# The order of VectorE's work within one step of an interleaved 30-pass FFN

## The chip, the cores and the metric

The kernel runs on one core of a Trainium2 chip. The core has a matrix engine (TensorE, PE in the profile, with PEld for its weight loads), VectorE (DVE), ScalarE (ACT), GpSimd (POOL) and SyncE (SP), each with its own instruction queue worked in order, and 16 DMA engines. The metric is the device time of one execution in microseconds (us), lower is better; the median of three runs of the kernel before is 4197.89 us (4197.65 to 4198.25).

## The reference

One layer of a graph network over 12500 nodes with 256 features in float32. A graph convolution and a linear attention are added to the input; then a feed-forward recurrence of 30 passes is applied to every node. Cut to what matters here:

```python
xn = _layernorm(x)
x = x + relu(segment_sum((xn @ weight)[src] * edge_weight, dst)) + linear_attention(xn)

def step(h, _):                       # 30 times
    h = h + 0.01 * jnp.tanh(h)
    h = h * jax.nn.sigmoid(h)         # silu
    h = _layernorm(h, ln_w, ln_b)
    h = jnp.einsum('bsc,dc->bsd', h, W) + b
    return (h, None)

x = x + scan(step, _layernorm(x), length=30)
```

The rows are independent in the 30 passes. Within a row each pass needs the one before it.

## The kernel before

The 12500 nodes lie in 98 tiles of 128 rows, and these in 25 groups of four tiles (the last group has two). The kernel first norms x, builds edge lists and the attention's sums; from about 0.42 ms on, one long loop mixes everything that is left: the attention's product (`mix`) and the convolution's product (`W`) of each group, the edge sums that feed it, and the 750 passes (25 groups by 30).

A planner, `plan()`, lists the steps of that loop in the program beforehand. Each step has at most one item: `mix`, `W` or a `pass` of one group. Up to five groups are in their passes at once (ABREAST), two passes of one group stand at least four steps apart (APART), and a step may also hold two quads of edge sums, some gathers, and the joining of a new group. The list has 803 steps: 750 passes, 25 `mix`, 23 `W` and 5 empty ones. The instructions are then written in the order of the loop, and that order is kept on each engine's queue (`manual_schedule`).

A pass is a software pipeline over steps. If the pass is the item of step k:

- before it, `normed` (L1017 on, its instruction at L1022) makes z, the normed activations, with four VectorE instructions, one a tile. It is written in the first step in which the group's statistics exist and its pass is one or two steps ahead.
- step k: `transposes` on TensorE (L1036, into `pt`), and `copies` on ScalarE (L1043, to `zT`).
- step k+1: `matrix`, 16 matmuls (L1049) into `po`, of which there are two buffers.
- step k+2: `act1`, a Tanh on ScalarE (L995); `act2`, on VectorE s = 0.01 * tanh + h (L1001) and on ScalarE the Silu (L1002); `stats`, two `bn_stats` on VectorE (L1008) and on GpSimd ve (L1012) and rs, a power (L1014).

After the 30th pass the result is added to the base rows instead (L1108) and sent out by SyncE's queue. `mix` and `W` items end two steps later with sums on VectorE (L1114, L1123, L1124).

At the top of a step VectorE gets the selection matrices of coming quads (`selections`, L210 to L223) and clears a slot of the edge sums (L276). ScalarE copies the quads' sums (L247) and the finished slot (L275) ahead of the Tanh. GpSimd's gathers (L184) are written after the matmuls, behind the rs of the step before and ahead of this step's ve.

A group joins over six steps, held in the list `fresh` by the step k3 of its start: statistics of its base rows (L1174, L1178, L1180) in k3 and k3+1, its first norm (L1146, L1153, L1157) and Tanh in k3+2 and k3+3, its `act2` in k3+4, its `stats` at the end of k3+5.

So VectorE's order in a step of before is: selections, clearing; s of the pass two steps back (or a sum into the base); a joining group's s; z of the passes due in the next two steps; a joining group's first norm; the `bn_stats` of the pass two steps back; a joining group's statistics.

Of the kernel before, what the change touches and what calls it, by code (L numbers as in the profile page):

```python
# [31 lines left out]
def gps_layer(  # L32
# [252 lines left out]
    class KeyValue:  # L285
# [19 lines left out]
        def normed(self):  # L305
            rs8 = kvw.tile([P, 2 * HEADS], F32, name="rs8")
            nc.vector.reciprocal(rs8, self.sd)
            nc.vector.tensor_tensor(
                kns[self.t % 3][:, :, :D], self.pkv, rs8[:, :, None].to_broadcast([P, 2 * HEADS, D]), ALU.mult
            )  # L310
# [315 lines left out]
    with tc.If(n_out > 0):  # L626
        with ExitStack() as pg_:
# [12 lines left out]
            for t in range(NE):  # L640
# [8 lines left out]
                d = gp.tile([P, 1], F32, name="d")  # L649
                nc.vector.tensor_copy(d[:rows], d_i[:rows])  # L650
                d = d[:rows]
# [333 lines left out]
    norm, zs, zTs, pos, xts, first_norm = {}, {}, {}, {}, {}, {}  # L985
# [3 lines left out]
    def flat(h, nt):  # L989
        return h[:, : nt // 2].rearrange("p q c j -> p (q c j)")  # L990
# [7 lines left out]
    def act2(gi, h, s):  # L998
        nt = groups[gi][1]
        sf = flat(s, nt)  # L1000
        nc.vector.scalar_tensor_tensor(sf, sf, 0.01, flat(h, nt), op0=ALU.mult, op1=ALU.add)  # L1001
        nc.scalar.activation(sf, sf, AF.Silu)  # L1002

    def stats(gi, s):
        t0, nt = groups[gi]
        st = hp.tile([P, G // 2, 6], F32, name="st")
        for q in range(nt // 2):
            nc.vector.bn_stats(st[:, q, :], s[:, q].rearrange("p c j -> p (c j)"))  # L1008

        sv = st.rearrange("p q (j f) -> p (q j) f", f=3)  # L1010
        ve = fp.tile([P, G], F32, name="ve")
        nc.gpsimd.tensor_scalar(ve[:, :nt], sv[:, :nt, 2], 1.0 / C, EPS, ALU.mult, ALU.add)  # L1012
        rs = hp.tile([P, G], F32, name="rs")
        nc.gpsimd.tensor_tensor(rs[:, :nt], ve[:, :nt], mhalf[:, :nt], ALU.pow)  # L1014
        norm[gi] = (s, sv, rs)
# [41 lines left out]
    item = lambda k: steps[k][0] if 0 <= k < K and steps[k][0] else (None, None)  # L1057
    quads_of = lambda k: steps[k][1] if k < K else 0
    fresh = []
    written = {}  # L1060
    selections(ed.summed + quads_of(0) - ed.selected)
    for k in range(K + 3):
        nq = quads_of(k)

        selections(ed.summed + nq + quads_of(k + 1) - ed.selected)
        copy_quads()
        free_nodes()
        kind, gi = item(k)[:2]
        if kind in ("mix", "W"):
            t0, nt = groups[gi]  # L1070
            xts[kind, gi] = fp.tile([P, G, C], F32, name="xt")
            if kind == "mix":
                load_rows(x, xts[kind, gi], t0, nt, nc.sync)
            else:
                rows = accw[bass.ds(n_out * ((G + t0) * P), nt * P), :]
                nc.sync.dma_start(out=xts[kind, gi][:, :nt, :], in_=rows.rearrange("(g p) c -> p g c", p=P))

        if kind == "pass":
            transposes(gi)
        kind1, g1 = item(k - 1)[:2]  # L1080

        if kind1 == "pass":
            zT, _ = zTs.pop(g1)
            pos[kind1, g1] = matrix(groups[g1][1], lambda j, k: zT[:, j, k, :], w2, True)
        elif kind1 == "mix":
            pos[kind1, g1] = matrix(groups[g1][1], lambda j, k: xnT[g1][:, j, k, :], mix)
        elif kind1 == "W":
            aT = ed.aT.pop(g1)
            pos[kind1, g1] = matrix(groups[g1][1], lambda j, k: aT[:, k, j * P : (j + 1) * P], wg)
        add_quads()  # L1090
        gathers(steps[k][3] if k < K else 0)
        for _ in range(nq):
            sum_quad()

        kind2, g2 = item(k - 2)[:2]
        last = kind2 == "pass" and item(k - 2)[2] == FFN_ITERS - 1
        if kind2 == "pass" and not last:
            s2 = act1(g2, pos[kind2, g2])
        if kind == "pass":
            copies(gi)  # L1100
        if kind2 == "pass" and not last:
            act2(g2, pos.pop((kind2, g2)), s2)
        elif last:
            t0, nt = groups[g2]
            for q in range(nt // 2):
                h = pos[kind2, g2][:, q].rearrange("p c j -> p j c")
                r = slice(2 * q, 2 * q + 2)
                nc.vector.tensor_tensor(base[g2][:, r, :], h, base[g2][:, r, :], ALU.add)  # L1108
            pos.pop((kind2, g2))
            rows_io(out, base[g2], t0, nt, False, nc.sync)  # L1110
            written[g2] = k
        elif kind2 == "mix":
            nt = groups[g2][1]
            nc.vector.tensor_tensor(base[g2], pos.pop((kind2, g2))[:, :nt, :], xts.pop((kind2, g2))[:, :nt, :], ALU.add)  # L1114
            if g2 < ed.weighted:
                aT = ed.aT.pop(g2).rearrange("p k (g n) -> p k g n", n=P)
                for i in range(KC):
                    bk = base[g2][:, :, i * P : (i + 1) * P]
                    nc.vector.scalar_tensor_tensor(bk, aT[:, i], 0.0, bk, op0=ALU.max, op1=ALU.add)
        elif kind2 == "W":  # L1120
            nt = groups[g2][1]
            ac = xts.pop((kind2, g2))[:, :nt, :]
            nc.vector.tensor_tensor(ac, pos.pop((kind2, g2))[:, :nt, :], ac, ALU.add)  # L1123
            nc.vector.scalar_tensor_tensor(base[g2], ac, 0.0, base[g2], op0=ALU.max, op1=ALU.add)  # L1124

        for g3, k3 in fresh:
            if k == k3 + 4:
                act2(g3, *first_norm[g3])  # L1130
        for d in (1, 2):
            kind3, g3 = item(k + d)[:2]
            if kind3 == "pass" and g3 in norm:
                normed(g3)
        for g3, k3 in fresh:
            nt = groups[g3][1]
            if k in (k3 + 2, k3 + 3):
                mv, rs = first_norm[g3, "stats"]
                if k == k3 + 2:

                    if 0 in written and written[0] + 2 <= k:
                        h = base[0].rearrange("p g c -> p (g c)").rearrange("p (q c j) -> p q c j", c=C, j=2)
                    else:
                        h = fp.tile([P, G // 2, C, 2], F32, name="z", bufs=3)
                    sh = fp.tile([P, G], F32, name="f_ve")
                    nc.vector.scalar_tensor_tensor(  # L1146
                        sh[:, :nt], mv[:, :nt, 0], -1.0, rs[:, :nt], op0=ALU.mult, op1=ALU.mult
                    )
                    first_norm[g3, "h"] = (h, sh)
                h, sh = first_norm[g3, "h"]  # L1150
                q = k - k3 - 2
                if 2 * q < nt:
                    nc.scalar.activation(  # L1153
                        h[:, q, :, 0], base[g3][:, 2 * q, :], AF.Identity, bias=sh[:, 2 * q : 2 * q + 1],
                        scale=rs[:, 2 * q : 2 * q + 1],
                    )
                    nc.vector.tensor_scalar(  # L1157
                        h[:, q, :, 1], base[g3][:, 2 * q + 1, :], mv[:, 2 * q + 1, 0:1], rs[:, 2 * q + 1 : 2 * q + 2],
                        ALU.subtract, ALU.mult,
                    )  # L1160
                if k == k3 + 3:
                    first_norm[g3] = (h, act1(g3, h))
        if kind2 == "pass" and not last:
            stats(g2, s2)
        start = steps[k][2] if k < K else None
        if start is not None:
            fresh.append((start, k))
        for g3, k3 in list(fresh):
            nt = groups[g3][1]
            if k == k3:  # L1170
                first_norm[g3, "st"] = fp.tile([P, G, 6], F32, name="f_st")
            for j in range(nt):
                if j // 2 == k - k3:
                    nc.vector.bn_stats(first_norm[g3, "st"][:, j, :], base[g3][:, j, :])  # L1174
            if k == k3 + 1:
                mv = fp.tile([P, G, 2], F32, name="f_mv")
                for j in range(nt):
                    nc.vector.bn_aggr(mv[:, j, :], first_norm[g3, "st"][:, j, :])  # L1178
                ve = fp.tile([P, G], F32, name="f_ve")
                nc.vector.tensor_scalar(ve[:, :nt], mv[:, :nt, 1], 1.0, EPS, ALU.mult, ALU.add)  # L1180
                rs = fp.tile([P, G], F32, name="f_rs")
                nc.gpsimd.tensor_tensor(rs[:, :nt], ve[:, :nt], mhalf[:, :nt], ALU.pow)
                first_norm[g3, "stats"] = (mv, rs)
            elif k == k3 + 5:
                stats(g3, first_norm[g3][1])
                fresh.remove((g3, k3))
# [31 lines left out]
```

## Time and profile before

| | |
|---|---|
| median of 3 runs | 4197.89 us |
| profiled execution, its time | 4203.52 us |
| its span | 4201.7 us |
| granted TensorE clock, mean | 0.99 |
| z (L1022), 2940 instructions | 1033.1 us busy |
| st (L1008), 1470 | 938.1 us busy |
| s (L1001) out of po, 725 | 863.8 us busy |
| Silu (L1002), 750 | 780.5 us busy |
| Tanh (L995) out of po, 725 | 729.7 us busy |
| rs (L1014), 750 | 763.7 us busy |
| gathers (L184), 1563 | 1596.3 us busy |

A line of the timeline gives the start, the length, engine, line, operation, the tile written and those read, the shapes and how many instructions are merged; in brackets the idle time before it and what ended it. A line of the waits gives who waited for whom, the total, how many times and the longest. A line of the windows gives the stretch, its length, the busy time of PE, PEld, DVE, ACT and POOL (with the number of instructions), the granted clock, the DMA share and GB/s.

### The profile page before, as it was taken

What the parts mean: (1) busy time and instruction counts of PE and PEld (TensorE: products, weight loads), DVE (VectorE), ACT (ScalarE), POOL (GpSimd) and SP (SyncE); (2) the same over time, 40 slices, a digit from 0 to 9 for tenths busy, and PEclk for the clock granted to TensorE, in tenths of its full rate; (3) what the DMA queues carried; (4) which work ended last, traced back from release to release, by engine and by line L of the source; (5) the groups of instructions that cost most, each with busy time, mean ns of one, the idle gap of its engine ahead of it and who ended that gap; (6) DMA issues with size and microseconds to landing.
All of it is one profiled execution on the core that took longest, in us unless ns stands there. A gap on an engine that the chain in (4) does not pass through costs nothing.

```text
span 4201.7 us, 68013 instructions
## 1 busy us (share of the span) xinstructions
PE 4074.6 (97%) x24201; PEld 3383.3 (81%) x24201; DVE 3400.9 (81%) x7393; ACT 2525.7 (60%) x3762; POOL 2575.3 (61%) x3186
## 2 busy tenths in 40 slices
PE   8797999999999999999999999999999999999999
PEld 4444778888888888888888888888888888888888
DVE  8454578888888888888888888888888888888887
ACT  7332246666666666666666666666666665667775
POOL 3464666777777777777777777777667652222222
PEclk9899999999999999999999999999999999999999
DMA  8322532222222222222222222222222210000000
GB/s 261 102 87 71 154 97 66 64 62 64 76 61 71 75 64 72 72 66 71 72 64 72 78 64 72 71 73 60 72 70 59 64 49 14 6 6 1 1 1 23
DMA packets 147687, 278.36 MB, mean 66 GB/s; under 512 B 28047, under 2 KB 97197, under 8 KB 147341
## 3 DMA queue, kind: packets, MB, share of 16 engines
q0 software_dynamic: 75024, 204.97, 16.8%
q1 hardware_dynamic: 72173, 68.42, 5.3%
q8 instruction: 197, 3.23, 0.3%
q14 instruction: 149, 1.22, 0.1%
q10 hardware_dynamic: 144, 0.52, 0.0%
HBM read 247.68 MB, written 26.12 MB: 65 GB/s over the span
## 4 chain that ended last, share of the span: by engine, by line
PE 77%; DVE 11%; ACT 3%; issue 3%; POOL 2%; another core or an unknown queue 1%; DMA 0%; POOLq 0%; ACTq 0%; DVEq 0%
PE po L1049 53%; PE pt L1036 13%; PE pq L236 4%; DVE z L1022 4%; PE pa L261 3%; PE pkv L290 3%; DVE st L1008 3%; DVE s L1001 2%; ACT s L995 1%; POOL rs L1014 1%; PE pacc L316 1%; ACT s L1002 1%; POOL xg L184 0%; DVE big L1108 0%
## 5 line engine op out<-in xcount | busy, mean ns | idle before, releaser
L1049 PE MATMUL po<-w,zT 128*128 128x256 f32 x11760 | 2670.7, 380 | 3.7 <-ACT zT L1043 1.8
L1049 PEld LDWEIGHTS po<-w,zT 128*128 128x128 f32 x11760 | 2179.6, 190 | 282.9 <-issue 7.8
L184 POOL DMA_INDIRECT xg<-xnd,src_i x1563 | 1596.3, 1021 | 529.8 <-issue 317.6
L1002 ACT ACTIVATE s<-s 128x1024 f32<-128x1024 f32 (+1 forms) x750 | 780.5, 1041 | 580.2 <-DVE s L1001 561.3
L1022 DVE TENSOR_SCALAR z<-s,st,rs 128x256 f32<-128x256 f32 x2940 | 1033.1, 417 | 94.5 <-POOL rs L1014 90.8
L1008 DVE BATCH_NORM_STATS2 st<-s 128x6 f32<-128x512 f32 x1470 | 938.1, 679 | 181.8 <-ACT s L1002 163.6
L1001 DVE SCALAR_TENSOR_TENSOR s<-s,po 128x1024 f32<-128x1024 f32 x725 | 863.8, 1192 | 269.1 <-ACT s L995 207.0
L995 ACT ACTIVATE s<-po 128x1024 f32<-128x1024 f32 x725 | 729.7, 1007 | 216.8 <-PE po L1049 205.6
L1043 ACT ACTIVATE zT<-pt 128x512 f32<-128x512 f32 x1470 | 801.8, 602 | 60.9 <-PE pt L1036 57.3
L1036 PE MATMUL pt<-ident,z 128*128 128x128 f32 x5880 | 793.9, 276 | 36.1 <-DVE z L1022 34.3
L1036 PEld LDWEIGHTS pt<-ident,z 128*128 128x128 f32 x5880 | 671.1, 142 | 174.7 <-issue 78.6
L1014 POOL TENSOR_TENSOR rs<-ve,mhalf 128x4 f32<-128x4 f32 (+1 forms) x750 | 763.7, 1018 | 62.5
L1012 POOL TENSOR_SCALAR ve<-st 128x4 f32<-128x4 f32 (+1 forms) x750 | 146.8, 196 | 946.5 <-DVE st L1008 899.3
L247 ACT COPY sq<-pq 128x256 f32<-128x256 f32 x196 | 72.4, 370 | 296.2 <-PE pq L236 196.1
L236 PE MATMUL pq<-xg,sel 128*32 128x256 f32 x3126 | 224.0, 386 | 9.1 <-issue 7.0
L290 PE MATMUL pkv<-wkv,big 128*128 128x512 f32 x392 | 199.3, 631 | 10.2 <-issue 5.4
L261 PE MATMUL pa<-selq,sq 128*128 128x192 f32 (+2 forms) x1168 | 182.7, 293 | 13.6 <-ACT sq L247 9.2
L261 PEld LDWEIGHTS pa<-selq,sq 128*128 128x128 f32 x1168 | 170.8, 192 | 25.0 <-ACT sq L247 10.0
L275 ACT COPY aT<-pa 128x128 f32<-128x128 f32 x196 | 51.5, 263 | 213.9 <-PE pa L261 147.3
L236 PEld LDWEIGHTS pq<-xg,sel 128*32 128x32 f32 x3126 | 84.9, 109 | 112.8 <-issue 71.9
L301 DVE TENSOR_REDUCE v<-sq 128x8 f32<-128x512 f32 x98 | 66.8, 682 | 95.1 <-ACT sq L297 77.8
L290 PEld LDWEIGHTS pkv<-wkv,big 128*128 128x128 f32 x392 | 70.3, 198 | 67.4 <-issue 57.6
(154 smaller groups left out, 1532.0 us busy)
## 6 DMA issues: line engine op xcount, KB each, us to landing
xg<-xnd,src_i POOLq DMA_INDIRECT x1563
xt<-in_x_dram SPq DMA_DIRECT2D x48, 512.0 KB
xnd<-xt SPq DMA_DIRECT2D x24, 512.0 KB
out_dram<-big SPq DMA_DIRECT2D x24, 512.0 KB
xt<-accw SPq DMA_DIRECT2D x22, 512.0 KB
ac<-accw SPq DMA_DIRECT2D x2, 512.0 KB
xg<-in_dst_dram SPq DMA_DIRECT2D x6, 128.0 KB
xg<-in_src_dram SPq DMA_DIRECT2D x6, 128.0 KB
```

The costliest lines, as they stand in the source:

```text
L184: nc.gpsimd.indirect_dma_start(out=ed.xg[t], out_offset=None, in_=xnd, in_offset=bass.IndirectOffsetOnAxis(ap=src_i[:, t : t + 1], axis=0),)
L236: nc.tensor.matmul(ed.pq[j * 2 * WIN : (j + 1) * 2 * WIN, :], lhsT=sel[:, j, :], rhs=ed.xg.pop(q * Q + j), start=(q % 2 == 0), stop=last, ...
L261: nc.tensor.matmul(pa[:, k, c : c + hi - lo], lhsT=sq[:rows, k * P : (k + 1) * P], rhs=selq[:rows, lo - n0 : hi - n0], start=False, stop=( ...
L995: nc.scalar.activation(flat(s, nt), flat(h, nt), AF.Tanh)
L1001: nc.vector.scalar_tensor_tensor(sf, sf, 0.01, flat(h, nt), op0=ALU.mult, op1=ALU.add)
L1002: nc.scalar.activation(sf, sf, AF.Silu)
L1008: nc.vector.bn_stats(st[:, q, :], s[:, q].rearrange("p c j -> p (c j)"))
L1014: nc.gpsimd.tensor_tensor(rs[:, :nt], ve[:, :nt], mhalf[:, :nt], ALU.pow)
L1022: nc.vector.tensor_scalar(z[:, j, :], s[:, j // 2, :, j % 2], sv[:, j, 1:2], rs[:, j : j + 1], ALU.subtract, ALU.mult)
L1036: nc.tensor.transpose(pt[:, i, k, :], z[:, 2 * q + i, k * P : (k + 1) * P], ident)
L1043: nc.scalar.activation(zT[:, 2 * q : 2 * q + 2], pt, AF.Copy, bias=1.0)
L1049: nc.tensor.matmul(po[:, j // 2, :, j % 2] if paired else po[:, j, :], lhsT=lhsT(j, k), rhs=rhs[:, k, :], start=(k == 0 and (j % 2 == 0 or ...
```

## The change

Two blocks of the loop are moved; no instruction is added or taken away. The block that norms the passes due in the next two steps goes from behind the activations' sums to ahead of them, directly after TensorE's work of the step is written. The sum of a joining group (with its Silu) goes from ahead of the norms to behind the statistics of the pass two steps back.

```diff
@@ -1092,6 +1092,11 @@
         for _ in range(nq):
             sum_quad()
 
+        for d in (1, 2):
+            kind3, g3 = item(k + d)[:2]
+            if kind3 == "pass" and g3 in norm:
+                normed(g3)
+
         kind2, g2 = item(k - 2)[:2]
         last = kind2 == "pass" and item(k - 2)[2] == FFN_ITERS - 1
         if kind2 == "pass" and not last:
@@ -1126,13 +1131,6 @@
 
 
         for g3, k3 in fresh:
-            if k == k3 + 4:
-                act2(g3, *first_norm[g3])
-        for d in (1, 2):
-            kind3, g3 = item(k + d)[:2]
-            if kind3 == "pass" and g3 in norm:
-                normed(g3)
-        for g3, k3 in fresh:
             nt = groups[g3][1]
             if k in (k3 + 2, k3 + 3):
                 mv, rs = first_norm[g3, "stats"]
@@ -1162,6 +1160,9 @@
                     first_norm[g3] = (h, act1(g3, h))
         if kind2 == "pass" and not last:
             stats(g2, s2)
+        for g3, k3 in fresh:
+            if k == k3 + 4:
+                act2(g3, *first_norm[g3])
         start = steps[k][2] if k < K else None
         if start is not None:
             fresh.append((start, k))
```

VectorE's order in a step becomes: selections, clearing; z of the passes due in the next two steps; s of the pass two steps back (or a sum into the base); a joining group's first norm; the `bn_stats` of the pass two steps back; a joining group's s; a joining group's statistics.

## The prediction

> **What bounds the kernel now.** I read four views: the page (busy shares, chain), the windows over the long stage, the timeline, and the waits of VectorE and TensorE. First the page and the window from 640 to 4177 us.
>
> ```profile
> span 4201.7 us, 68013 instructions
> PE 4074.6 (97%) x24201; PEld 3383.3 (81%) x24201; DVE 3400.9 (81%) x7393; ACT 2525.7 (60%) x3762; POOL 2575.3 (61%) x3186
> PE 77%; DVE 11%; ACT 3%; issue 3%; POOL 2%; another core or an unknown queue 1%; DMA 0%; POOLq 0%; ACTq 0%; DVEq 0%
> 640.00:4177.00 3537.00, 3504.01 (x20999) 3007.25 (x20998) 3000.01 (x6298) 2269.57 (x3242) 2223.29 (x2754) 1.00 0.19 55
> ```
>
> The chain of work that ended last runs mainly on PE, and in the window PE is busy 3504 of 3537 us at clock 1.00, DVE 3000. So PE sets the pace and DVE has 537 us to spare. What matters is how those spare microseconds are arranged, and that is read in the timeline. Two stretches: a steady one with gathers, and a late one with gaps in it.
>
> ```profile
> 2009.54 1.27 DVE L1008 BATCH_NORM_STATS2 st<-s 128x6 f32<-128x512 f32 x2
> 2010.90 0.19 POOL L1012 TENSOR_SCALAR ve<-st 128x4 f32<-128x4 f32 x1
> 2011.18 1.04 POOL L1014 TENSOR_TENSOR rs<-ve,mhalf 128x4 f32<-128x4 f32 x1
> 2012.08 1.21 DVE L1001 SCALAR_TENSOR_TENSOR s<-s,po 128x1024 f32<-128x1024 f32 x1
> 2013.20 1.38 DVE L1022 TENSOR_SCALAR z<-s,st,rs 128x256 f32<-128x256 f32 x4
> 2014.48 1.28 DVE L1008 BATCH_NORM_STATS2 st<-s 128x6 f32<-128x512 f32 x2
> ```
> ```profile
> 3882.11 1.22 DVE L1001 SCALAR_TENSOR_TENSOR s<-s,po 128x1024 f32<-128x1024 f32 x1
> ...
> 3883.36 1.06 ACT L1002 ACTIVATE s<-s 128x1024 f32<-128x1024 f32 x1 [0.31 <-DVE s L1001]
> ...
> 3884.45 1.29 DVE L1008 BATCH_NORM_STATS2 st<-s 128x6 f32<-128x512 f32 x2 [1.12 <-ACT s L1002]
> ...
> 3885.83 0.20 POOL L1012 TENSOR_SCALAR ve<-st 128x4 f32<-128x4 f32 x1 [2.38 <-DVE st L1008]
> 3886.11 1.01 POOL L1014 TENSOR_TENSOR rs<-ve,mhalf 128x4 f32<-128x4 f32 x1
> ...
> 3887.15 1.39 DVE L1022 TENSOR_SCALAR z<-s,st,rs 128x256 f32<-128x256 f32 x4 [0.82 <-POOL rs L1014]
> ```
>
> A step's DVE work is a ring: s feeds the Silu on ACT, the Silu feeds the statistics st, st feeds ve and rs on POOL, rs feeds z. The first stretch shows the order of before hiding both hand-overs: while POOL makes rs (2010.90 to 2012.22) DVE works on selections and s; while ACT does the Silu, DVE does z, and st starts with no gap. The second stretch shows both hand-overs bare: no z is due behind s at 3882.11, so st idles 1.12 us for the Silu, and z at 3887.15 comes 1.41 us after st ended at 3885.74, although a half-size s lies between. The waits:
>
> ```profile
> DVE s L1001 <- ACT s L995: 207.0, 212, 5.2
> DVE st L1008 <- ACT s L1002: 163.6, 155, 1.9
> DVE z L1022 <- POOL rs L1014: 90.8, 214, 2.1
> PE pt L1036 <- DVE z L1022: 34.3, 39, 2.4
> ```
>
> Columns are total us, times, longest. DVE's largest wait is for the Tanh, that is for PE. PE waited for z only 34.3 us in all, so the most that earlier z's can give back is about that.
>
> **The change part by part.** It adds and removes no instruction, and what it moves issues no DMA and nothing on POOL or SP; a moved sum carries one Silu on ACT.
>
> (1) Norms to the front of the step. The z's now stand on DVE ahead of s, and behind the statistics of the step before. A pass at step k has its statistics at step k+2, and at step k+3 a z is due if the group's next pass is at k+4 or k+5. The planner keeps passes of a group at least 4 steps apart and has five groups abreast, so that is the usual case. I followed the planner's list through the loop: 803 steps, 750 passes (725 with s and st), 750 z's; 565 z's fall in the step right after their statistics, in 549 different steps. In each of those DVE now meets st, then z, with only selections between, and waits the whole 1.41 us for rs. And s no longer has a z behind it: each st waits the 1.12 us of the Silu, as at 3884.45. So both covers go at once, and DVE's ring closes once a step:
> z to s 1.30 (2013.20 to 2014.48 is 1.28, 3887.15 to the next DVE instruction 1.31) + s to st uncovered 2.34 (3882.11 to 3884.45) + st 1.28 + st's end to z 1.41 = 6.33 us, against 4.71 us that a step takes now (3554 us over the 754 steps number 40 to 793, whose ends follow).
>
> The sum from step 40 (its matmuls begin at 622.6) to step 793 (DVE's first last-pass sum of the tail, 4176.7); ranks in the plan counted, prices from the timeline rows:
> - s, Silu, st: 679 x (2.34 + 1.28) = 2458; the last group has half the tiles: 28 x (1.38 + 0.69) = 58, from its rows at 4188 to 4190 us (s, 1.38 later st of 0.69)
> - z: 700 x 1.30 = 910; half-size 28 x 0.65 = 18 (six z parts take 2.03, four 1.38)
> - waits for rs: 504 x 1.41 = 711; half-size 27 x 1.09 = 29 (st ends 4161.60, ve 4161.69, rs 4161.97 for 0.69)
> - sums into the base in steps that have no s: 6 x 1.13 + 21 x 2.38 + 20 x 1.20 = 81
> - selections of a pair of quads, 1.27 each: about 110 pairs fall in steps with an rs wait and lie inside its 1.41, so they cost nothing; the other 51 cost 65. If the cover were absent: 140 more.
> - 167 steps have no z; there s follows st so soon that the Tanh, queued on ACT behind the Silu and sometimes a copy, is late: about 20.
> Together 4350 (2516 + 928 + 740 + 81 + 65 + 20).
>
> (2) A joining group's sum (s and Silu) at the end of the step, 22 joinings in this stretch. Its DVE 1.13 lies in the rs wait of the next step in 21 cases, but its Silu (1.06) now stands on ACT ahead of the next Tanh (1.02) with st already done: from the end of st 1.25 + 1.06 + 1.05 = 3.4 until s may start, against 1.41 + 1.30 = 2.7. The bounds are 0 and 22 x 1.2; I take 26, the side of the rows. The joining group's own st at the end of the step costs 22 x 1.20 = 26, and its other statistics 10 that no rs wait covers. Together 62.
>
> (3) POOL. Behind rs it issues gathers, some 1.26 from one to the next (2008.56, 2009.82), mostly two or three a step. In a 6.33 us step three fit (3.8 us) before the next ve is due 4.9 us after rs. In a step without z (3.62 us) they do not, and rs comes late for the following z. The trace of before does not run at this pace; bounds 0 and one gather for each of some 120 such steps, 150 us; I take 40, since two gathers just fit with the small waits of (1).
>
> (4) PE. z earlier gives at most its 34.3 us, and that only if PE were still the bound. PE needs about 4.7 us a step, the ring 4452 / 754 = 5.9 on the mean, so PE idles some 1.2 us a step and the gain is nothing. PSUM: s and the base sums free the matmul's buffers later on DVE; two buffers give two rings, 11 us, for 3.6 us of matmuls and 1.05 of Tanh, so it costs nothing; without that cover up to the ring again.
>
> Sum: 622.6 + 4350 + 62 + 40 + 25 (4176.7 to 4201.7, the end, unchanged) = 5100 us of span, 898 above 4201.7. The profiled execution took 4203.5, 5.6 above the median of 4197.9; the same difference gives 4197.9 + 898, about **5095 us**, a factor 1.21.
>
> Two rules were weighed against this. In the page's first lines PE is the fullest engine, and DVE has a fifth of its time free. The Trainium skill (Perfetto Trace Analysis, Identifying the Most-Contended Engine) ranks engines by occupancy and would have PE optimised first, from which an order on DVE should be worth about nothing, and 4198 us would stay. The timeline's ring decides otherwise for me. The second is the clock. The granted clock in the rows:
>
> ```profile
> 340.00:360.00 20.00, 16.98 (x99) 9.47 (x100) 11.59 (x30) 6.33 (x16) 12.26 (x14) 1.00 0.29 85
> 400.00:420.00 20.00, 15.69 (x91) 12.68 (x92) 9.54 (x26) 0.64 (x2) 6.08 (x7) 0.78 0.23 61
> 420.00:440.00 20.00, 15.28 (x51) 7.68 (x50) 0.17 (x1) 0.90 (x4) 12.77 (x14) 0.65 0.42 128
> ```
>
> With short gaps and PE 85% busy the clock is 1.00; around and after a 12.8 us idle stretch (before 403.7) it is 0.78 and 0.65. The new PE gaps are short, under 2 us, so I take 1.00. The Trainium skill (TensorE: Matmul & The Clock Gate, HAM oscillation) puts the limit at idle gaps of about 3.4 us, and by that too nothing is added; at the half rate that it states for longer gaps PE would need 9.4 us a step and bind.
>
> **The rivals.**
> - POOL late everywhere (0.13): a gather, 1.26 us, stands before ve in the steps with an rs wait, as where st ended at 2004.45 and ve came at 2005.68. In half of them 549/2 x 1.26 = 345 more, 5440; in all 5790. Against it: the longer step has room.
> - Half the rs waits covered (0.10): if more than selections lay between st and z, 0.5 x 740 less, about 4725. For it: joinings and base sums; against it: they are counted, and are few.
> - The clock falls (0.03). PE would bind below 4.71 / 5.9 = 0.80 of full clock. At 0.65 it is 7.25 us a step, 754 x 1.35 = 1020 more, about 6110.
> - Not slower (0.03), the other side: rs is ready before z is reached. Then z's at the front cost nothing, PE's 34.3 us of waiting for z goes, and the time is 4164. My sum has 740 us of rs waits and 780 for Silu and Tanh, 2.0 us a step, and 3.9 for the rest of the ring; it decides where ring and PE are equal, at 0.8 us of waits a step. Against it: DVE already waits 90.8 us for rs in spite of an s in between.
>
> **How the numbers follow.** The forecast has 0.71; its own range is 4980 to 5230, from (2) and (3) at their bounds and the tanh waits of the steps without z at 0 to 0.5 us each. To leave out no more than 2 in 10 the range goes to 4900, part of the way to the covered case, and 5370, a POOL late in about two fifths of the steps. Within 0.2% (8 us, about what can be told from no change here) I give 0.01, faster 0.02, slower 0.97.
>
> **What would show it.** In the profile after: PE busy share near 80%; idle before z put down to rs of some 600 to 750 us; idle before st put down to the Silu of some 750 us; DVE's wait for the Tanh small; the chain mainly on DVE, ACT and POOL; a timeline of z, s, gap 1.1, st, gap 1.4. It is wrong if z's do not wait for rs, if the Silu is still covered, or if the clock column falls.

## The result, and the profile after

The changed kernel takes 5176.1 us (median of 4; 5170.85 to 5178.91), the kernel before 4198.1 beside it: a ratio of 1.2325, 95% interval 1.2311 to 1.2339, 978 us slower. The forecast was 5095, with a range of 4900 to 5370. The profiled execution took 5175.53 us, its span is 5173.7.

The page of the changed kernel, the lines that answer to those shown of before (span, busy times, and the chain by engine and by line):

```profile
span 5173.7 us, 67124 instructions
PE 4397.8 (85%) x24201; PEld 3496.6 (68%) x24201; DVE 3437.6 (66%) x7393; ACT 2471.5 (48%) x3762; POOL 2617.9 (51%) x3186
DVE 47%; POOL 16%; PE 15%; ACT 12%; issue 6%; another core or an unknown queue 0%; POOLq 0%; DMA 0%; DVEq 0%; ACTq 0%
DVE z L1022 17%; DVE st L1008 14%; DVE s L1001 13%; ACT s L1002 11%; POOL rs L1014 10%; PE po L1049 9%; POOL xg L184 3%; POOL ve L1012 2%; PE pkv L290 2%; PE pq L236 1%; PE pt L1036 1%; PE pa L261 1%; PE pacc L316 1%; ACT s L995 0%; DVE sel L215 0%
```

The chain was on TensorE for 77% of the span; now z, st and s on VectorE, the Silu on ScalarE and rs on GpSimd hold 65% of it. The work has hardly changed (VectorE 3437.6 us busy against 3400.9). What is new is waiting, as VectorE's waits show (total us, times, longest):

```profile
DVE st L1008 <- ACT s L1002: 782.8, 711, 1.1
DVE z L1022 <- POOL rs L1014: 636.6, 489, 3.0
...
DVE s L1001 <- ACT s L995: 40.1, 28, 3.1
```

Before, these three were 163.6, 90.8 and 207.0. VectorE hardly waits any more for TensorE's product by way of the Tanh (40.1 us); it waits in nearly every step for the Silu (711 times, 1.10 us each) and in 489 steps for rs (1.30 us each). A late stretch of the changed kernel's timeline shows one turn:

```profile
4899.77 1.38 DVE L1022 TENSOR_SCALAR z<-s,st,rs 128x256 f32<-128x256 f32 x4 [1.41 <-POOL rs L1014]
...
4901.06 1.22 DVE L1001 SCALAR_TENSOR_TENSOR s<-s,po 128x1024 f32<-128x1024 f32 x1
4902.31 1.06 ACT L1002 ACTIVATE s<-s 128x1024 f32<-128x1024 f32 x1 [3.68 <-DVE s L1001]
...
4903.40 1.29 DVE L1008 BATCH_NORM_STATS2 st<-s 128x6 f32<-128x512 f32 x2 [1.12 <-ACT s L1002]
...
4904.77 0.20 POOL L1012 TENSOR_SCALAR ve<-st 128x4 f32<-128x4 f32 x1 [5.04 <-DVE st L1008]
...
4905.06 1.01 POOL L1014 TENSOR_TENSOR rs<-ve,mhalf 128x4 f32<-128x4 f32 x1
4906.10 1.38 DVE L1022 TENSOR_SCALAR z<-s,st,rs 128x256 f32<-128x256 f32 x4 [1.41 <-POOL rs L1014]
```

From z to z it is 4906.10 - 4899.77 = 6.33 us, and each instruction in it starts when the one above is done; s alone does not need the z above it, it stands behind it in VectorE's queue. TensorE's main wait is the other side of it: its output buffers stay full until the late s reads them (before, all idle time ahead of L1049 was 3.7 us).

```profile
PE po L1049 <- DVE s L1001: 526.0, 412, 3.8
PE pt L1036 <- DVE z L1022: 66.5, 87, 2.1
```

### The profile page after: what moved, and what is told of

Read it like the earlier page. It is cut to its first block, busy times and chain, and to the rows that moved or that the text cites. A ratio compares the mean times of both kernels' runs of the same rounds, so it can differ in the third digit from the quotient of the medians.

```text
span 5173.7 us, 67124 instructions
## 1 busy us (share of the span) xinstructions
PE 4397.8 (85%) x24201; PEld 3496.6 (68%) x24201; DVE 3437.6 (66%) x7393; ACT 2471.5 (48%) x3762; POOL 2617.9 (51%) x3186
## 4 chain that ended last, share of the span: by engine, by line
DVE 47%; POOL 16%; PE 15%; ACT 12%; issue 6%; another core or an unknown queue 0%; POOLq 0%; DMA 0%; DVEq 0%; ACTq 0%
DVE z L1022 17%; DVE st L1008 14%; DVE s L1001 13%; ACT s L1002 11%; POOL rs L1014 10%; PE po L1049 9%; POOL xg L184 3%; POOL ve L1012 2%; PE pkv L290 2%; PE pq L236 1%; PE pt L1036 1%; PE pa L261 1%; PE pacc L316 1%; ACT s L995 0%; DVE sel L215 0%
## 5 line engine op out<-in xcount | busy, mean ns | idle before, releaser
L1049 PE MATMUL po<-w,zT 128*128 128x256 f32 x11760 | 2874.5, 400 | 570.4 <-DVE s L1001 509.3
L1049 PEld LDWEIGHTS po<-w,zT 128*128 128x128 f32 x11760 | 2287.1, 200 | 1006.4 <-DVE s L1001 602.5
L184 POOL DMA_INDIRECT xg<-xnd,src_i x1563 | 1613.7, 1032 | 520.4 <-issue 281.4
L1012 POOL TENSOR_SCALAR ve<-st 128x4 f32<-128x4 f32 (+1 forms) x750 | 167.6, 224 | 1884.8 <-DVE st L1008 1867.2
L1036 PE MATMUL pt<-ident,z 128*128 128x128 f32 x5880 | 814.3, 278 | 98.0 <-DVE z L1022 66.5
L1001 DVE SCALAR_TENSOR_TENSOR s<-s,po 128x1024 f32<-128x1024 f32 x725 | 860.4, 1187 | 53.5 <-ACT s L995 40.1
L1036 PEld LDWEIGHTS pt<-ident,z 128*128 128x128 f32 x5880 | 657.5, 141 | 286.4 <-issue 173.8
L297 ACT ACTIVATE sq<-pkv 128x512 f32<-128x512 f32 x98 | 58.1, 593 | 108.1 <-PE pkv L290 38.0
```

The source lines that it names most:

```text
L184: nc.gpsimd.indirect_dma_start(out=ed.xg[t], out_offset=None, in_=xnd, in_offset=bass.IndirectOffsetOnAxis(ap=src_i[:, t : t + 1], axis=0),)
L1036: nc.tensor.transpose(pt[:, i, k, :], z[:, 2 * q + i, k * P : (k + 1) * P], ident)
L1049: nc.tensor.matmul(po[:, j // 2, :, j % 2] if paired else po[:, j, :], lhsT=lhsT(j, k), rhs=rhs[:, k, :], start=(k == 0 and (j % 2 == 0 or ...
```

## The experiments

The theory: the loss is the two hand-overs, 1.41 us to GpSimd and 1.12 us to ScalarE, that the new order leaves without other work of VectorE over them. Rivals: the joining group's sum breaks the order; TensorE's waits for its output buffers, or its clock, are the loss.

The record names chip 0 for the two single parts, for the norms behind the statistics and for the next step's norm alone, chip 1 for all other runs here, and no chip for the first pair. The kernel before has medians of 4100.35 us on chip 0 and 4101.02 and 4101.52 on chip 1, against 4198 in the first pair. The changed kernel itself was run again on chip 1 alone, 5087 us, and is compared with the runs of both. The expectations of those four runs were written with 4198 and 5176 in mind, so their differences are compared, not their absolute times.

**The two kernels again.** The changed kernel and the kernel before were run unedited, on chip 1 (the single parts that the first expectation speaks of ran on chip 0).

> The changed kernel itself again, beside the single parts on the chip that they ran on. Theory (ring): the norms at the front, 5068 there, and the joining sum, 37 alone, roughly add: 5085 to 5105. Rival (the clock or the chip decides): another ratio than 1.2325 by over 0.02.

> The kernel before itself, for a profile from the chip of the experiments, where it takes 4100 us and not 4198. Theory (the difference lies ahead of the loop, in the stage that loads lists and makes keys and values): the loop from its second W product to its first sum of the tail takes 3568 us as on the first chip, within 5. Rival: the loop itself is shorter by tens of us.

The changed kernel took 5087.25 us, a ratio of 1.2406 (1.2388 to 1.2424), 986 us slower. The kernel before was profiled at 4100.24 us, 103 below its first profile. I compare the loop from its second W product to the first sum of the tail: 3567.9 us in the first profile, 3555.7 here. That is 12 us, more than the 5 expected, so neither side of this expectation held in full, but it is far from the 103. Of the rest, 91 us lie ahead of that product (it starts at 517.95 instead of 608.72). So the loop's loss can be compared: 4536.5 - 3567.9 = 969 us in the first pair, 4530.1 - 3555.7 = 974 here.

**Each part alone.** Only the norms at the front:

```diff
+        for d in (1, 2):
+            kind3, g3 = item(k + d)[:2]
+            if kind3 == "pass" and g3 in norm:
+                normed(g3)
+
         kind2, g2 = item(k - 2)[:2]
...
-        for d in (1, 2):
-            kind3, g3 = item(k + d)[:2]
-            if kind3 == "pass" and g3 in norm:
-                normed(g3)
```

> Only the norms move to the front; a joining group's sum stays where it was. Theory (the ring: each step waits 1.41 us for rs and 1.12 us for the Silu): nearly all of the loss stays, 5120 to 5165 us, 10 to 50 below the full change. Rival (the joining sum's Silu, late on ScalarE ahead of the next Tanh, is what breaks the order): below 4700.

Only the joining sum at the end:

```diff
-        for g3, k3 in fresh:
-            if k == k3 + 4:
-                act2(g3, *first_norm[g3])
...
         if kind2 == "pass" and not last:
             stats(g2, s2)
+        for g3, k3 in fresh:
+            if k == k3 + 4:
+                act2(g3, *first_norm[g3])
```

> Only a joining group's sum moves to the end of its step; the norms stay behind s. Theory (ring): 25 joinings by at most 1.2 us and TensorE's spare time over it, 4198 to 4225. Rival (the joining sum is what breaks the order): above 4600.

The norms alone: 5068.13 us, ratio 1.2361 (1.2340 to 1.2381), 19 below the whole change, as expected; the two parts alone add up to 1005, near the 986 of both. The joining sum alone: 4137.43 us, ratio 1.0091 (1.0074 to 1.0108), 37 us, 10 more than the upper end expected. So the norms make 968 of the 986 us and the first rival falls. In that second run VectorE's waits for the Tanh rose from 244.1 to 284.4 us and TensorE's for z from 26.1 to 47.7, against the profile of the kernel before on chip 1; how much of either reaches the end was not traced.

**The two hand-overs apart.** The norms behind the statistics of the step, for the same passes:

```diff
-        for d in (1, 2):
-            kind3, g3 = item(k + d)[:2]
-            if kind3 == "pass" and g3 in norm:
-                normed(g3)
+        due = [g3 for kind3, g3, *_ in (item(k + d) for d in (1, 2)) if kind3 == "pass" and g3 in norm]
...
         if kind2 == "pass" and not last:
             stats(g2, s2)
+        for g3 in due:
+            normed(g3)
```

> The same norms, due in the next two steps, are written behind the statistics of the step: s, st, z. rs then has s, the Silu's wait and st for cover; the Silu has none, as in the change. It separates the two hand-overs. Theory (ring): s to st 2.34 + st 1.28 + z 1.30 = 4.92 us plus 0.27 for selections a step against TensorE's 4.71; from the terms of the prediction 2516 + 928 + 81 + 206 + 62 + 20 = 3813 against 3554, so 4460 us, and up to 4700 if z, now at the end of a step, comes late for the 271 passes in the very next step. Rival (TensorE stands because s frees the matmul buffers late, behind z): s is as early in its step as before, so 4200 to 4250.

It took 4464.47 us, ratio 1.0888 (1.0870 to 1.0906), 364 above before, inside the 262 to 502 of the theory. The groups of this run's page show the separation (after the bar: busy, mean ns of one, then the idle time before them and its releaser):

```profile
L1008 DVE BATCH_NORM_STATS2 st<-s 128x6 f32<-128x512 f32 x1470 | 946.6, 685 | 772.0 <-ACT s L1002 772.0
L1022 DVE TENSOR_SCALAR z<-s,st,rs 128x256 f32<-128x256 f32 x2940 | 1008.8, 410 | 0.3 <-POOL rs L1014 0.3
```

The wait for the Silu is whole, that for rs is gone, and the loss is 364 us instead of 986. TensorE's waits for z rose to 217.7 us, the lateness that the upper end allowed for.

**Fewer waits for rs.** The changed kernel with z at the front for the next step's pass alone:

```diff
-        for d in (1, 2):
+        for d in (1,):
```

> The changed kernel, but z at the front is written only for the pass of the next step, not for that of the step after it. By the plan 271 z's then still follow their statistics by one step, against 565. Theory (ring): some 278 steps lose their 1.41 us wait, -392, and some 60 pairs of selections lose their cover, +70: about 4855. Rival (the matmul buffers that s frees late): s stands behind as many z's as before, so about 5176.

4682.53 us, ratio 1.1424 (1.1405 to 1.1443): 405 below the changed kernel, where 321 was expected. Its waits for rs fell from 640.3 to 304.4 us, 336 of the 405; those for the Tanh fell by 24, and the other 45 were not traced. The rival's "as the change" is far off.

**The GpSimd hand-over made longer.** ve is written twice, 0.28 us more between st and rs, in either kernel:

```diff
         nc.gpsimd.tensor_scalar(ve[:, :nt], sv[:, :nt, 2], 1.0 / C, EPS, ALU.mult, ALU.add)
+        nc.gpsimd.tensor_scalar(ve[:, :nt], sv[:, :nt, 2], 1.0 / C, EPS, ALU.mult, ALU.add)
```

> The changed kernel with ve written twice by GpSimd before rs: 0.28 us more from st to z. Theory (ring): the hand-over to GpSimd lies on the path in some 490 steps, so 490 x 0.28 = 137 us more than the change (between 110 and 155). Rival (the matmul buffers that s frees late, or the clock): nothing is added, within 20 us of the change.

> The kernel before with ve written twice: the same 0.28 us. Theory (ring): there s and the selections cover it and TensorE has the pace, so 0 to 25 us over the kernel before. Rival (the hand-over was never covered, and the change only makes it longer): 100 or more.

In the changed kernel: 5263.21 us, 176 more, with the waits for rs at 815.2 us against 640.3: the added wait, 175 us, is as large as the added time. That it is added decides against the rival, but the size is a miss, above the 110 to 155 expected: 0.28 us for the 491 waits of the changed kernel would be 137, and now 537 z's wait. Where the rest of the added wait comes from was not traced. In the kernel before: 4175.79 us, 74 more, ratio 1.0181 (1.0165 to 1.0196). That is a miss too, between the 0 to 25 of the theory and the 100 or more of the rival. VectorE's waits there, double ve first, the kernel before below (on the same chip):

```profile
DVE z L1023 <- POOL rs L1015: 275.5, 371, 3.2
```
```profile
DVE z L1022 <- POOL rs L1014: 93.0, 216, 2.1
```

There are 182 us more of waiting for rs, and 74 more at the end. The cover of before was not complete: with 0.28 us more on GpSimd, 155 more z's wait for rs.

**TensorE taken off.** The changed kernel with half the product of each pass:

```diff
-            for k in range(KC):
+            for k in range(1 if paired else KC):
                 nc.tensor.matmul(
...
-                    start=(k == 0 and (j % 2 == 0 or not paired)), stop=(k == KC - 1), skip_group_check=paired,
+                    start=(k == 0 and (j % 2 == 0 or not paired)), stop=(paired or k == KC - 1), skip_group_check=paired,
```

> The changed kernel with one of the two matmuls of each pass's product left out (half of the features are not summed in the 30 passes). TensorE's work falls by 5880 x 0.227 = 1335 us. Theory (ring): TensorE is off the path in the loop, so the time falls only where the loop starts, by 0 to 80 us. Rival (TensorE's 526 us of waits for its output buffers and its lower clock are part of the loss): the time falls by 300 us or more.

5075.32 us, 12 below the changed kernel, in the theory's 0 to 80. TensorE has 5880 matmuls fewer and its mean granted clock is 0.844, and one turn of VectorE is still 4709.37 - 4703.04 = 6.33 us:

```profile
4703.04 1.29 DVE L1008 BATCH_NORM_STATS2 st<-s 128x6 f32<-128x512 f32 x2 [1.12 <-ACT s L1002]
...
4708.31 3.78 PE L1049 MATMUL po<-w,zT 128*128 128x256 f32 x8 [1.87 <-DVE s L1001]
...
4709.37 1.29 DVE L1008 BATCH_NORM_STATS2 st<-s 128x6 f32<-128x512 f32 x2 [1.12 <-ACT s L1002]
```

Eight matmuls take 3.78 us here and cost nothing. So neither TensorE's waits for its output buffers nor its clock make the loss.

**Norms first where no Silu needs cover.** The kernel before with the norms at the front of those steps alone that have no s; in a second version only the next step's norm, with the distances (1,) handed to the first of the two calls and (1, 2) to the second.

```diff
+        def norms_due():
+            for d in (1, 2):
+                kind3, g3 = item(k + d)[:2]
+                if kind3 == "pass" and g3 in norm:
+                    normed(g3)
+
...
         last = kind2 == "pass" and item(k - 2)[2] == FFN_ITERS - 1
+        if kind2 != "pass" or last:
+            norms_due()
...
-        for d in (1, 2):
-            kind3, g3 = item(k + d)[:2]
-            if kind3 == "pass" and g3 in norm:
-                normed(g3)
+        norms_due()
```

> The kernel before, with the norms at the front of a step only where no s and no statistics follow in it (some 80 steps with a sum into the base or nothing). Theory (ring): there is no Silu there to cover, TensorE gets those z's 1.2 to 2.4 us earlier and its 34 us of waits for z shrink: 0 to 20 us below the kernel before. Rival (the base sums, now later, free the matmul buffers late): 5 to 30 above.

> As the run that put norms to the front only where no s follows, but only for the pass of the very next step; the z of the step after it stays behind the base sums. Theory (there the base sums came late and held the matmul buffers, 28 us of TensorE's waits, against 15 us gained on z): fewer base sums are delayed, so -10 to +10 against the kernel before. Rival (the next step's z in front is itself the loss): 20 to 30 above, as there.

The first: 4130.24 us, ratio 1.0069 (1.0055 to 1.0083), 29 above before; the rival was right. TensorE's waits for z fell from 26.1 to 19.3 us, but it now waits for the sums into the base, which hold its output buffers:

```profile
PE pt L1036 <- DVE z L1022: 19.3, 27, 1.8
PE po L1049 <- DVE big L1116: 11.1, 9, 2.1
PE po L1049 <- DVE big L1122: 9.9, 8, 2.0
...
PE po L1049 <- DVE xt L1131: 7.4, 6, 2.5
```

The second: 4107.40 us, ratio 1.0014 (1.0005 to 1.0023), 6 above. TensorE's waits for the two sums named `big` fell from 21.0 to 4.6 us, so most of the 29 was the z of the step after next, made ahead of a sum that TensorE needed sooner. No version beat the kernel before.

## Why the prediction was right

**The ring and its two prices held.** The forecast had a turn of 6.33 us; the late stretch has 6.33. The price of 1.41 us from st to z, read from before's line at 3887.15, stands again at 4906.10, and the 1.12 for the Silu almost everywhere. That the new order exposes both at once is shown by the two runs that took away waits for rs, all of them (norms behind the statistics) or about half (only the next step's norm): the time fell by 623 and 405 us.

**The count held.** 549 steps were to wait for rs. The profile has 489 such waits, since selections fill the whole time in some; in the summed stretch they make 622.9 us, where 740 and 40 for GpSimd, less the 140 of selections inside, 640 in all, were expected.

**The sum came out 74 us short** in the span (5100 against 5173.7). The loop's part was 622.6 + 4452; it ran from 629.1 to 5151.35, so 70 us too little for the loop, 6 at its start, and the end 3 us shorter. One term mis-sized was the ring's price in the stretch with gathers, which I had taken from both stretches as one. z to s is 1.34 us there on the mean (324 pairs) and 1.29 later (80 pairs), and the hand-over to GpSimd 1.45. One turn there, in the changed kernel:

```profile
688.10 1.43 DVE L1022 TENSOR_SCALAR z<-s,st,rs 128x256 f32<-128x256 f32 x4 [1.45 <-POOL rs L1014]
689.45 1.20 DVE L1001 SCALAR_TENSOR_TENSOR s<-s,po 128x1024 f32<-128x1024 f32 x1
691.77 1.29 DVE L1008 BATCH_NORM_STATS2 st<-s 128x6 f32<-128x512 f32 x2 [1.12 <-ACT s L1002]
694.50 1.43 DVE L1022 TENSOR_SCALAR z<-s,st,rs 128x256 f32<-128x256 f32 x4 [1.44 <-POOL rs L1014]
```

That is 6.40 us. For 552 z's the 0.04 make 22 us, and the 0.04 of the hand-over in some 300 steps 12: about half of the 70. The sum also leaves out the clearing of slots (164 in the stretch, 27 us busy) and charges 10 us for the joining groups' statistics and first norms, which keep VectorE busy for 65; how much of both lies inside waits for rs was not separated, and the remainder was not traced.

**GpSimd late** was costed at 40 us, a choice between 0 and 150: 58 waits for rs are longer than 1.55 us, together 41 us above 1.43, so the size was in part luck. The mechanism was as forecast. Fifteen of these waits last about 2.9 us, and 14 of the 15 come right after a step without z. In one of them the step without z runs from s at 782.69 to the end of st at 786.31; a gather ends at 787.96, ve starts at 788.03 and z at 789.39, so a gather stood before ve. The rival that put a gather in front everywhere did not come.

**The joining sum** was costed at 26 us for its late Silu. On top of the norms it cost 19; on its own 37, a case that the forecast did not price.

**The clock** was a miss of detail. I took gaps under 2 us and a clock of 1.00; the mean granted clock was 0.959, and 0.90 in the last 174 us. It did not matter, since the ring has the pace, as the run with half the matmuls shows at 0.844. In the loop (629 to 5151 us) the clock is 0.96, and TensorE has 578 gaps over 0.15 us there, 1.17 on the mean, 37 of them over 2 us and one over 3.4, of 3.80. The Trainium skill (TensorE: Matmul & The Clock Gate, HAM oscillation) gives idle gaps beyond about 3.4 us as the cause of a lower clock. Only one gap of the loop is that long, and the clock is lower all the same; what lowered it was not tried.

**That TensorE's output buffers cost nothing** was right for the time, with the wrong picture: two buffers were to cover the late s, but TensorE did wait 526 us for them, and simply had the time.

**The range.** The forecast's own range of 4980 to 5230 does not follow from the bounds that it names: 0 to 26 us for the late Silu, 0 to 150 for GpSimd and 0 to 83 for the Tanh, around 5095, give about 5010 to 5270. The 5176 lies in both.

**The rule of occupancy.** The Trainium skill (Perfetto Trace Analysis, Identifying the Most-Contended Engine) has the engine of the highest occupancy optimised first, which the prediction read from TensorE's 97%; but for TensorE the section asks for the share of peak FLOPs and of weight loads instead of the busy share of its matmuls. The weight loads are busy for 81% of the kernel before, the same share as VectorE, so that by this measure the two were level. The measurement goes against reading an 81% busy engine as one with time to spare: with 1% more busy time (3437.6 us against 3400.9), and by order alone, a ring through VectorE became the bound.

## What to carry to other kernels

On an engine that works its queue in order, write the turn of dependences once round and ask at each hand-over what the engine does meanwhile; price an exposed hand-over from a place in the trace where it already stands bare, and multiply by the number of turns. Free time of an engine is not cover in itself: an instruction moved to the front because it is "due first" takes the cover from where it stood and may wait where it goes. Before moving work ahead of anything that frees a buffer, ask who is waiting for that buffer.

## What the runs showed that was not expected

- A cover can be a matter of a fraction of a microsecond. In the kernel before, 0.28 us more on GpSimd, an engine 61% busy, cost 74 us, and 25 joining sums moved within their step cost 37.
- The same kernel took 4198 us in the first pair and 4100 to 4102 in the later runs, on two chips. 91 us of it lie ahead of the loop's second W product. Between 100 and 200 us TensorE was busy for 75.8 us at clock 0.83 in the first profile, 91.8 us at 0.97 in the later one. What makes the difference was not tried.
- VectorE's z takes some 4% longer in the stretch with gathers than behind it (1.34 us for four against 1.29). The cause was not tried.
